# The last block of a two-layer FFN kernel: another order of the last down sums, smaller last stores, and smaller down-weight loads

## The chip, the cores and the metric

The kernel runs on one core of one Trainium2 chip. The metric is the device time of one execution in microseconds; where a kernel was timed several times, the median of its runs.

A core has five engines with queues of their own: TensorE (PE in the profile; its weight loads are listed as PEld), VectorE (DVE), ScalarE (ACT), GpSimd (POOL) and SyncE (SP). Transfers are issued here from the queues of SP, ACT and POOL and are moved by 16 DMA engines.

## The reference, cut to what matters

Two layers, each a residual around a feed-forward network whose input is first transformed per batch. All the change touches is the last product of the second layer and the final sum:

```python
def _L1_ffn_ref(x, ln_w, gate_w, up_w, down_w):
    var = jnp.mean(jnp.square(x), axis=-1, keepdims=True)
    nx = x * jax.lax.rsqrt(var + RMS_EPS) * ln_w
    g = jnp.einsum('bsh,ih->bsi', nx, gate_w)
    u = jnp.einsum('bsh,ih->bsi', nx, up_w)
    return jnp.einsum('bsi,hi->bsh', jax.nn.silu(g) * u, down_w)
x = x + _L0_ffn_ref(_L0_cond_ref(x, ...), ...)
x = x + _L1_ffn_ref(_L1_cond_ref(x, L1_cond_weight, itok_B_3_7), L1_ffn_ln_w, ...)
return x
```

x has 8 batches of 128 tokens with 512 features, 1024 tokens in all; the inner width of the second layer is 1792. The first layer's weights are 4-bit numbers with scales, the second layer's are float32.

## The kernel before, in words

**Layout.** Everything is held transposed: features on the 128 partitions, the 1024 tokens along the free dimension, in two halves tb = 0 and 1 of 512 (TB). The residual and result `xT` has four chunks m of 128 features (KC = 4); the inner width of the second layer is 14 chunks j of 128.

**Products in three sums.** A float32 product is made from reduced-precision (fp32r) parts. Weight and activation are each split into H (high), L (low, scaled) and D (a difference of the two). A bank of PSUM first gets all products of parts 0 and 1 (the H and L sums), is multiplied by a constant in place (`rescale`, lines 174 to 181, which picks ACT or DVE by a planner's account of their load), and then gets the products of part 2 (D) on top. `done` (L1138, on DVE) adds the bank, times a constant, to `xT`.

**Blocks.** The second layer's inner chunks are worked in four blocks, `BLOCKS1` = (0, 4), (4, 8), (8, 11), (11, 14). In each, gate and up (L1056) are made for its chunks j, with the splitting of later weights put between by the planner, then `down(j0, j1)` (matmuls L1121) adds the block's part to all four output chunks. In the middle of a block, `load_down` issues the loads of its down weights on SP (L1103), in pairs of chunks of 512 KB and a single one where the number is odd; `prepare_down` queues their splitting: ACT reads the raw weights (L940, L943), DVE makes the other parts (L949, L952). Loads of gate and up weights (`load_wgu`, L932) go through the same SP queue.

**The order of the work.** The instructions of PE, DVE and ACT run in the order in which the program writes them; each waits by semaphores for what it reads. Transfers from SP and ACT take one of eight completion counters in turn; a transfer that takes a counter again first waits for the one that had it before. At the program's end SP checks the counters one after another, in a fixed order.

**The last block.** With chunks 11 to 13, each sum of H and L over one tb is 2 x 3 = 6 matmuls, each D sum 3. The order of the 72 matmuls is: H and L of output chunks 0, 1, 2 (36 in all, rescaled as they end); D of chunks 0 and 1 (`added`, 6 each), each followed by `done` over 1024 columns and two stores of 512 columns (L1142; tb 0 from ACT's queue, tb 1 from SP's); H and L of chunk 3, tb 0 then tb 1, each with its rescale; D of chunk 2 with `done` and two stores; D of chunk 3 for tb 0, `done`, store; the same for tb 1. The core of it (L1147 and after):

```python
m = KC - 1
banks[m, 1] = pair("down")[:, 1]
for tb in tbs:
    passes(m, (tb,), every, (0, 1))
    rescale(banks[m, tb], HLSCALE)
added(m - 1)
for tb in tbs:
    store(m - 1, tb)
for tb in tbs:
    passes(m, (tb,), every, (2,))
    done(m, xT[:, m, tb * TB : (tb + 1) * TB], banks[m, tb])
    store(m, tb)
```

After the last instruction every engine takes a branch (L1228) over a second version of the network, which inputs of this kind do not need, to the program's end (L1371), where SP checks the counters and the engines meet.

Of the kernel before, what the change touches and what calls it, by code (L numbers as in the profile page):

```python
# [13 lines left out]
F32 = mybir.dt.float32  # L14
# [5 lines left out]
AF = mybir.ActivationFunctionType  # L20
ALU = mybir.AluOpType

P = 128
B, T, D = 8, 128, 512
NT = B * T
TB = 512
# [36 lines left out]
HLSCALE = -(1.0 + EPS) / EPS  # L63
# [32 lines left out]
def network_in(ctx, tc, a, out, by_groups, flag, again):  # L96
    nc = tc.nc
# [4 lines left out]
    def pair(name):  # L102
        return psum.tile([P, 2, 512], F32, tag="ps", name=name)
# [9 lines left out]
    xT = const.tile([P, KC, NT], F32, name="xT")  # L113
# [19 lines left out]
    def charge(engine, us):  # L133
        load[engine] = max(load[engine], clock[0] + AFTER) + us

    def took(engine, n):

        return 0.1 + n / 1000 if engine == "act" else 0.15 + n / 950
# [29 lines left out]
    def spent(n):  # L168

        base = clock[0]  # L170
        clock[0] += 0.2326 * n
        pump(base, clock[0] + OVER)

    def rescale(ps, by):
        n = ps.free_size()
        engine = min(load, key=lambda e: max(load[e], clock[0] + AFTER) + took(e, n))
        charge(engine, took(engine, n))
        if engine == "act":
            nc.scalar.activation(ps, ps, AF.Copy, scale=by)  # L179
        else:  # L180
            nc.vector.tensor_scalar(ps, ps, by, None, ALU.mult)
# [39 lines left out]
    for b in range(B):  # L221
        (nc.scalar, nc.sync)[b % 2].dma_start(
            out=xb[:, b].rearrange("p c t -> p (c t)"), in_=a["xb"][b]
# [7 lines left out]
    at = np.cumsum((0,) + SMALLS)  # L231
# [221 lines left out]
    def by_groups_of_scales():  # L453
# [243 lines left out]
        with tc.manual_schedule(engines={EngineType.PE, EngineType.DVE, EngineType.Activation}):  # L697
# [64 lines left out]
            pools["w1"] = w1_stack.enter_context(tc.tile_pool(name="w1", bufs=1, side="right"))  # L762
            hp = h_stack.enter_context(tc.tile_pool(name="h0", bufs=1, side="right"))
            load_down(*BLOCKS0[0])
            for pair0 in PAIRS0[2:4]:
                load_qw(*pair0)
# [17 lines left out]
            gate_up_pair(2, 3)  # L784
            flush("d0")
            load_down(*BLOCKS0[1])
            dequantise(PAIRS0[3])
            queue_down(*BLOCKS0[1], "d4", at=clock[0] + 6.0)
            down(*BLOCKS0[0])
            ready(PAIRS0[2])  # L790
            load_qw(*PAIRS0[4])
            gate_up_pair(4, 5)
            ready(PAIRS0[3])
            load_qw(*PAIRS0[5])
            flush("d4")
            load_down(*BLOCKS0[2])
            dequantise(PAIRS0[4], (8, 10))
            gate_up_pair(6, 7)
            dequantise(PAIRS0[5], (10, 11))
            queue_down(*BLOCKS0[2], "d8")  # L800
            queue("dve", "indices", 1.7, indices)
            down(*BLOCKS0[1])
            flush("indices")
            first_w1()
# [291 lines left out]
            queue_split(f"h{j}", h, h3[j])  # L1096

    def load_down(j0, j1):
        raws = {}
        for k0 in range(j0, j1, 2):  # L1100
            k1 = min(k0 + 2, j1)
            raws[k0, k1] = fd.tile([P, 2, D], F32, tag="wd", bufs=2, name="wd1")[:, : k1 - k0]
            nc.sync.dma_start(out=raws[k0, k1], in_=a["wd1"][:, k0:k1, :])  # L1103
        return raws

    def prepare_down(raws):
# [6 lines left out]
    def down(j0, j1):  # L1113

        sums = [pair("down") for _ in range(KC)]
        banks = {(m, tb): sums[m][:, tb] for m in range(KC) for tb in range(NTB)}
        last = j1 == NJ1

        def one(m, tb, j, which):
            for i in which:  # L1120
                nc.tensor.matmul(  # L1121
                    banks[m, tb],
                    lhsT=d3[j][i][:, m * P : (m + 1) * P],
                    rhs=h3[j][i][:, tb],
                    start=(i == 0 and j == j0),
                    stop=(j == j1 - 1 and i != 0),
                    skip_group_check=(i == 2),
                )
            spent(len(which))

        def passes(m, tbs, js, which):
            for tb in tbs:
                for j in js:
                    one(m, tb, j, which)

        def done(m, x, ps):
            charge("dve", took("dve", ps.free_size()))
            nc.vector.scalar_tensor_tensor(x, ps, -EPS, x, ALU.mult, ALU.add)  # L1138

        def store(m, tb):  # L1140
            cols = slice(tb * TB, (tb + 1) * TB)
            (nc.scalar, nc.sync)[tb].dma_start(out=out[m * P : (m + 1) * P, cols], in_=xT[:, m, cols])  # L1142

        tbs, every = range(NTB), range(j0, j1)

        def first(m):
            passes(m, tbs, range(j0, j1 - 1), (0, 1))  # L1147

        def ended(m):

            passes(m, tbs, range(j1 - 1, j1), (0, 1))
            rescale(sums[m], HLSCALE)

        def added(m):
            passes(m, tbs, every, (2,))
            done(m, xT[:, m, :].rearrange("p (b t) -> p b t", b=NTB), sums[m])

        if last:


            for fn in (first, ended):
                for m in range(KC - 1):
                    fn(m)
            for m in range(KC - 2):
                added(m)
# [3 lines that stand above are left out]
            banks[m, 1] = pair("down")[:, 1]  # L1169
            for tb in tbs:  # L1170
                passes(m, (tb,), every, (0, 1))
                rescale(banks[m, tb], HLSCALE)
            added(m - 1)
            for tb in tbs:
                store(m - 1, tb)
            for tb in tbs:
                passes(m, (tb,), every, (2,))
                done(m, xT[:, m, tb * TB : (tb + 1) * TB], banks[m, tb])
                store(m, tb)
            return  # L1180
        for fn in (first, ended, added):
            for m in range(KC):
                fn(m)

    with tc.manual_schedule(engines={EngineType.PE, EngineType.DVE, EngineType.Activation}):
        for j0, j1 in BLOCKS1:
            for j in range(j0, j1):
# [6 lines left out]
                if j == 0:  # L1194
# [5 lines left out]
                    fd = ctx.enter_context(tc.tile_pool(name="fd", bufs=1, side="left"))  # L1200
# [12 lines left out]
            if j1 == NJ1 and by_groups:  # L1213

                again.append(nc.values_load(flag[:1, :], min_val=0, max_val=1))
                tc.mark_branch_hint_location("again", hint=again[0], engines=FETCHED)
            down(j0, j1)


# [156 lines left out]
```

## Time and profile before

| what | value |
|---|---|
| median of 3 runs | 436.3 us (435.57 to 436.6) |
| the profiled execution's own time | 436.83 us |
| its span, from first to last instruction | 434.9 us |
| mean granted TensorE clock | 0.996 |
| PE busy | 424.8 us (98%), 1855 matmuls |
| DVE busy | 302.4 us (70%) |
| ACT busy | 232.0 us (53%) |
| down matmuls of layer 2 (L1121) | 336, 76.8 us, 389 ns each |
| transfers | 33.07 MB, 76 GB/s over the span |
| out stores (L1142) | 8 of 256 KB; 2.5 / 3.4 / 4.0 us to landing (least, median, most) |
| wd loads (L1103) | 6 of 512 KB (3.7 us to landing), 2 of 256 KB (2.6 us) |

The page belongs to one execution; its engines' rows give busy time, its chain the work that ended last, followed back from the end. A matmul lasts 389 ns but they overlap, so busy PE is not the same as PE at its peak. Times with a decimal point and no other mark are microseconds from the start of the span.

### The profile page before, as it was taken

The page shows a single profiled execution, that of the slowest core. Times are in us where ns is not written, and L with a number is a line of the kernel's source. Part 1 is how long each engine was busy: PE and PEld are TensorE (multiplying, and loading weights), DVE is VectorE, ACT ScalarE, POOL GpSimd, SP SyncE. Part 2 cuts the span into 40 slices and gives each one's busy share as a digit, 9 for nine tenths or more (in the row PEclk, how much of TensorE's full clock was granted, in tenths as well). Part 3 has the DMA queues.
Part 4 walks back from the last instruction along what each step waited for, and adds up shares of the span by engine and source line. Part 5 has one row for each costly group of instructions (what it writes and reads, how often), then busy time and mean ns, then how long its engine had stood idle before and what let it go on. Part 6 is the DMA issues. An engine that isn't in the chain of part 4 may idle for free.

```text
span 434.9 us, 4847 instructions
## 1 busy us (share of the span) xinstructions
PE 424.8 (98%) x1855; PEld 334.5 (77%) x1855; DVE 302.4 (70%) x432; ACT 232.0 (53%) x269; POOL 9.0 (2%) x20
## 2 busy tenths in 40 slices
PE   8999999999999999999999999999999999999992
PEld 8875778888888764447888888888888888888882
DVE  3998979998998769768179634679334676725552
ACT  5923899678877765347478132484132471425420
POOL 1000000000002001100000000000000000000000
PEclk9999999999999999999999999999999999999998
DMA  8931301010001505842114101132001110000013
GB/s 290 344 150 49 98 0 50 18 37 2 0 2 48 242 6 204 301 167 83 64 50 145 48 2 48 50 97 72 2 0 48 50 48 26 0 0 2 2 53 146
DMA packets 12094, 33.07 MB, mean 76 GB/s; under 512 B 1568, under 2 KB 4256, under 8 KB 11040
## 3 DMA queue, kind: packets, MB, share of 16 engines
q1 hardware_dynamic: 9760, 22.21, 15.3%
q0 software_dynamic: 1152, 8.39, 5.1%
q10 hardware_dynamic: 1152, 2.10, 1.3%
q8 instruction: 16, 0.26, 0.2%
q14 instruction: 14, 0.11, 0.1%
HBM read 30.59 MB, written 2.10 MB: 75 GB/s over the span
## 4 chain that ended last, share of the span: by engine, by line
PE 91%; DVE 4%; DMA 2%; ACT 1%; issue 0%; SPq 0%; ACTq 0%; DVEq 0%
PE gate L1056 18%; PE up L1056 18%; PE down L1121 17%; PE gate L539 9%; PE down L587 8%; PE up L539 8%; PE base L390 5%; PE adapt L999 5%; PE base L416 2%; DMA xb<-in_xb 2%; PE experts L293 1%; DVE xT L599 1%; PE nxT L1019 1%; ACT sl L555 1%; DVE h L558 1%; DVE w L952 1%
## 5 line engine op out<-in xcount | busy, mean ns | idle before, releaser
L1056 PE MATMUL gate<-a,w 128*128 128x512 f32 x336 | 81.8, 390 | 0.0
L1056 PE MATMUL up<-a,w 128*128 128x512 f32 x336 | 81.4, 389 | 0.0
L1121 PE MATMUL down<-h,d 128*128 128x512 f32 x336 | 76.8, 389 | 0.0
L1056 PEld LDWEIGHTS up<-a,w 128*128 128x128 f32 x336 | 63.1, 188 | 13.2
L1121 PEld LDWEIGHTS down<-h,d 128*128 128x128 f32 x336 | 63.1, 188 | 13.1
L1056 PEld LDWEIGHTS gate<-a,w 128*128 128x128 f32 x336 | 62.7, 188 | 13.5 <-ACT gate L179 0.6
L1073 DVE SCALAR_TENSOR_TENSOR h<-up,sl 128x1024 f32<-128x1024 f32 (+1 forms) x16 | 17.5, 1092 | 51.0 <-PE up L1056 44.6
L539 PE MATMUL gate<-a,dq 128*128 128x512 f32 (+1 forms) x176 | 47.7, 393 | 0.1
L539 PE MATMUL up<-a,dq 128*128 128x512 f32 (+1 forms) x176 | 47.4, 391 | 0.0
L587 PE MATMUL down<-h,wd 128*128 128x512 f32 (+1 forms) x176 | 42.3, 393 | 0.6 <-DVE h L193 0.4
L587 PEld LDWEIGHTS down<-h,wd 128*128 128x128 f32 (+1 forms) x176 | 32.5, 188 | 9.5 <-DVE h L193 0.9
L539 PEld LDWEIGHTS gate<-a,dq 128*128 128x128 f32 (+1 forms) x176 | 32.4, 185 | 8.4 <-ACT sl L555 0.6
L539 PEld LDWEIGHTS up<-a,dq 128*128 128x128 f32 (+1 forms) x176 | 32.4, 185 | 7.9 <-DVE a L671 0.3
L203 ACT ACTIVATE h<-h 128x1024 fp32r<-128x1024 f32 (+1 forms) x25 | 26.4, 1054 | 15.9 <-DVE h L1073 15.5
L1070 ACT ACTIVATE sl<-gate 128x1024 f32<-128x1024 f32 (+1 forms) x16 | 14.7, 919 | 35.8 <-PE gate L1056 35.8
L193 DVE TENSOR_TENSOR h<-h,h 128x1024 fp32r<-128x1024 f32 (+1 forms) x25 | 30.5, 1218 | 3.4 <-ACT h L203 3.4
L179 ACT ACTIVATE gate<-gate,ratio 128x1024 f32<-128x1024 f32 (+1 forms) x24 | 26.1, 1086 | 10.6 <-PE gate L539 10.6
L179 ACT ACTIVATE gate<-gate 128x1024 f32<-128x1024 f32 (+1 forms) x15 | 13.8, 923 | 30.8 <-PE gate L1056 30.8
L999 PE MATMUL adapt<-w,xT 128*128 128x512 f32 x64 | 28.9, 597 | 0.0
L179 ACT ACTIVATE down<-down 128x1024 f32<-128x1024 f32 (+1 forms) x10 | 9.2, 923 | 35.8 <-PE down L1121 35.8
L179 ACT ACTIVATE up<-up,ratio 128x1024 f32<-128x1024 f32 (+1 forms) x23 | 25.0, 1085 | 4.9 <-PE up L539 4.9
L1138 DVE SCALAR_TENSOR_TENSOR xT<-down,xT 128x1024 f32<-128x1024 f32 (+1 forms) x17 | 19.6, 1161 | 9.3 <-PE down L1121 9.1
(137 smaller groups left out, 482.6 us busy)
## 6 DMA issues: line engine op xcount, KB each, us to landing
wgu<-in_wgu SPq DMA_DIRECT2D x14, 512.0 KB, 3.3
wd<-in_wd SPq DMA_DIRECT2D x6, 512.0 KB, 3.7
qw<-in_qw_gu SPq DMA_DIRECT2D x5, 512.0 KB, 4.2
xT<-in_xT SPq DMA_DIRECT2D x2, 1024.0 KB, 11.6
xb<-in_xb ACTq DMA_DIRECT2D x4, 256.0 KB, 5.6
xb<-in_xb SPq DMA_DIRECT2D x4, 256.0 KB, 6.1
wT<-in_WT SPq DMA_DIRECT2D x4, 256.0 KB, 5.9
qwd<-in_qw_d SPq DMA_DIRECT2D x2, 512.0 KB, 8.2
```

Of the source, the lines that this page charges most:

```text
L179: nc.scalar.activation(ps, ps, AF.Copy, scale=by)
L193: nc.vector.tensor_tensor(lo, x, hi.bitcast(F32), ALU.subtract)
L203: nc.scalar.activation(hi, x, AF.Copy, scale=HSCALE)
L390: nc.tensor.matmul(base[m], lhsT=wT3[i][:, m, c * P : (c + 1) * P], rhs=x_parts(tb)[i][:, c, :], start=(i == 0 and c == 0), stop=(i == 1 a ...
L539: nc.tensor.matmul(ps, lhsT=dqs[j][:, c, half, :], rhs=a3[i][:, c, tb * TB : (tb + 1) * TB], start=(c == 0 and i == 0), stop=(i == 1), ski ...
L587: nc.tensor.matmul(ps[:, tb], lhsT=wds[k][:n, m * P : (m + 1) * P], rhs=h2[k][i][:, tb], start=(first and i == 0), stop=(i == 1), skip_gro ...
L999: nc.tensor.matmul(ps, lhsT=xT[:, c, b * T : (b + 1) * T], rhs=wt[:, c * D : (c + 1) * D], start=(c == 0), stop=(c == KC - 1),)
L1056: nc.tensor.matmul(ps, lhsT=w3[j][i][:, c, half * P : (half + 1) * P], rhs=a3[i][:, c, tb * TB : (tb + 1) * TB], start=(i == 2 and c == 0) ...
L1070: nc.scalar.activation(sl, ps, AF.Silu, scale=1.0 + EPS)
L1073: nc.vector.scalar_tensor_tensor(h, ps, 1.0 + EPS, sl, ALU.mult, ALU.mult)
L1121: nc.tensor.matmul(banks[m, tb], lhsT=d3[j][i][:, m * P : (m + 1) * P], rhs=h3[j][i][:, tb], start=(i == 0 and j == j0), stop=(j == j1 - 1 ...
L1138: nc.vector.scalar_tensor_tensor(x, ps, -EPS, x, ALU.mult, ALU.add)
```

## The change

Three edits, all in the second layer's `down`:

1. In the last block the D sum of output chunk 2 (with its `done` over 1024 columns) moves up, between the H and L sums of chunk 3 for tb 0 and those for tb 1. Its stores are issued after both. The two scalings of chunk 3 are written for ACT and no longer chosen by the planner.
2. The last output chunk is finished and stored in four pieces of 256 columns instead of two of 512. The queues of the stores are exchanged: tb 0 goes from SP, tb 1 from ACT.
3. The down weights of all blocks but the first are loaded one chunk (256 KB) at a time instead of in pairs; the tiles, and the instructions that read them, stay in pairs.

```diff
     def load_down(j0, j1):
         raws = {}
+        n = 2 if j0 == 0 else 1
         for k0 in range(j0, j1, 2):
             k1 = min(k0 + 2, j1)
-            raws[k0, k1] = fd.tile([P, 2, D], F32, tag="wd", bufs=2, name="wd1")[:, : k1 - k0]
-            nc.sync.dma_start(out=raws[k0, k1], in_=a["wd1"][:, k0:k1, :])
+            raw = raws[k0, k1] = fd.tile([P, 2, D], F32, tag="wd", bufs=2, name="wd1")[:, : k1 - k0]
+            for k in range(k0, k1, n):
+                nc.sync.dma_start(out=raw[:, k - k0 : k - k0 + n], in_=a["wd1"][:, k : k + n, :])
         return raws
...
-        def store(m, tb):
-            cols = slice(tb * TB, (tb + 1) * TB)
-            (nc.scalar, nc.sync)[tb].dma_start(out=out[m * P : (m + 1) * P, cols], in_=xT[:, m, cols])
+        def store(m, i, n=TB):
+            cols = slice(i * n, (i + 1) * n)
+            engine = (nc.sync, nc.scalar)[i * n // TB]
+            engine.dma_start(out=out[m * P : (m + 1) * P, cols], in_=xT[:, m, cols])
...
             banks[m, 1] = pair("down")[:, 1]
             for tb in tbs:
                 passes(m, (tb,), every, (0, 1))
-                rescale(banks[m, tb], HLSCALE)
-            added(m - 1)
-            for tb in tbs:
-                store(m - 1, tb)
+                nc.scalar.activation(banks[m, tb], banks[m, tb], AF.Copy, scale=HLSCALE)
+                if tb == 0:
+                    added(m - 1)
+            for t in tbs:
+                store(m - 1, t)
+            n = TB // 2
             for tb in tbs:
                 passes(m, (tb,), every, (2,))
-                done(m, xT[:, m, tb * TB : (tb + 1) * TB], banks[m, tb])
-                store(m, tb)
+                for i in range(TB // n):
+                    at = tb * TB + i * n
+                    done(m, xT[:, m, at : at + n], banks[m, tb][:, i * n : (i + 1) * n])
+                    store(m, at // n, n)
             return
```

## The prediction

> **What bounds the kernel now.** I read the busy slices of the page first, then the chain that ended last, then the last 15 us in small windows, then the single transfers and sequencer records behind the last vector operation.
>
> ```profile
> PE   8999999999999999999999999999999999999992
> PEclk9999999999999999999999999999999999999998
> DMA  8931301010001505842114101132001110000013
> ```
>
> ```profile
> 428.30:431.00 2.70, 0.00 (x0) 0.00 (x0) 0.00 (x0) 0.00 (x0) 0.00 (x0) 1.00 0.93 338
> 431.00:434.90 3.90, 0.00 (x0) 0.00 (x0) 0.00 (x0) 0.00 (x0) 0.00 (x0) 0.58 0.03 12
> ```
>
> By the page's 40 slices TensorE is full at a full clock until the last slice. The two rows of the windows table (length; busy time of PE, PEld, DVE, ACT, POOL; clock; DMA share; GB/s) show the rest: from 428.3 no engine computes, for 2.7 us the transfers run at 338 GB/s, and then 3.9 us pass with almost nothing moving. So the main part is worth nothing here unless it breaks, and the tail is 6.65 us long (428.3 to the span's end, 434.95).
>
> ```profile
> 410.81 14.97 PE down L1121 x66
> 425.78 0.03 issue
> 425.81 0.02 DVEq L1138
> 425.83 0.04 issue
> 425.87 1.39 DVE xT L1138 x2
> 427.26 0.35 issue
> 427.61 0.68 DVE xT L1138
> ```
>
> In the chain (start, length, what), 66 of the last 72 matmuls run without a gap, and then DVE ends it: the last six matmuls (to 427.12) hide behind DVE's 128x1024 addition of the third chunk. The last addition ends at 428.29.
>
> ```profile
> L1142 SPq DMA_DIRECT2D out<-xT x4: 332/335/348, 421.7 to 428.3; - x4
> L1142 ACTq DMA_DIRECT2D out<-xT x4: 338/369/382, 421.7 to 427.7; - x4
> DMA to landing us min/median/max: 2.5/3.4/4.0
> ...
> L1228 SPq EVENT_SEMAPHORE  x8: 17/17/17, 431.4 to 432.8; - x8
> L1228 ACTq COMPARE_BRANCH  x1: 68/68/68, 428.1 to 428.1; - x1
> L1228 DVEq EVENT_SEMAPHORE  x1: 21/21/21, 430.8 to 430.8; - x1
> L1228 ACTq EVENT_SEMAPHORE  x1: 17/17/17, 431.5 to 431.5; - x1
> ```
>
> Eight stores of 256 KB. Four are issued between 427.13 and 428.32: 1 MB is pending at once, and the DMA engines are saturated to 430.75, with two of the 16 late. The last store, issued at 428.32, lands at 432.29, the 4.0 of the row. SP's eight checks (431.4 to 432.8) are of the eight counters that the transfers take in turn: it waits for the second of them at 432.31, walks through the other six until 432.77, then through its other checks, and the span ends 2.66 us after the landing. Beside this, each engine leaves by a branch: ACT's is at 428.10 and its next instruction comes only at 431.55, 3.45 us later (DVE: 427.18 to 430.78, 3.60).
>
> **Part by part.** Times are on the trace's clock. Matmuls here start every 0.227 us; the third chunk's six D matmuls become numbers 55 to 60 of the 72 instead of 61 to 66.
>
> *Third chunk earlier.* Its last matmul ends at 424.41 instead of 425.77 (6 x 0.227 = 1.36). DVE has been idle since 422.95, starts the addition 0.1 later, ends at 425.73 instead of 427.10. Its two stores are no longer pending together with the last chunk's: SP issues at 425.76; ACT's sits behind ACT's second scaling and issues by 426.4 (bounds 425.86 and 426.4; it matters little). At the traced rate 512 KB take 1.4 us, from about 426.6 to 428.0.
>
> *A wait added.* Before, nine matmuls (2.04 us) lay between the end of tb1's H and L sums and its D; now three do. ACT starts scaling 0.04 us after the last H/L matmul, as at 424.44: 425.80, and takes 0.58, to 426.38. The weight load of tb1's first D waits for it, and its matmul follows 0.22 us after the load starts: 426.65 instead of 426.29. TensorE waits 0.37 us (bounds: 0.1 if the load were ahead, 0.5 with a slow semaphore) and ends at 427.50. Behind it are only tb1's three matmuls, DVE's two pieces, two stores.
>
> *Four additions for two.* 1024 columns take 1.225 us and 512 take 0.68, so 256 take about 0.41; starts are 1.14 and 0.60 apart, so pieces of 256 start 0.34 apart. Tb0: 426.55 and 426.89, to 427.30. Tb1: 427.57 and 427.91, to 428.32. Before: 428.29. The wait eats what the shorter DVE queue had gained: computing ends even, by 0.03.
>
> *Stores.* SP takes tb0's pieces (427.0, 427.33, both over before the next). ACT takes tb1's two: at its 0.37 per issue, 428.01 and 428.43, the second held 0.05 by the first and by a check of a counter, done at 428.80; its branch comes at 428.83. Before: SP at 428.32, ACT's branch 428.10. One issue more than before on each queue, so the last is issued 0.11 later. From issue to first packet was 0.82 (421.69 to 422.50): 429.25. A packet of 1,024 bytes takes 0.046 in this trace's records against 0.084 for 2,048; eight an engine are 0.37: 429.62. From last packet to landing 0.45: 430.07. The late engines carried 8 KB instruction fetches of 0.31 to 0.41 us each, and were 0.3 to 1.1 late; I keep 0.3 to 0.8: 430.4 to 430.9, where it was 432.29.
>
> Here a rule speaks against cutting. The trace has the 0.046 above. The Trainium skill, "DMA: Bandwidth & Descriptors", section Bandwidth, measured on loads of another issue path, advises transfers of 1 MiB or more[...]: 0.95 us for 64 KB, 6.15 for 1 MB. Between them 128 KB would be 1.30 (an estimate from that page). Two in a row from 428.83 would end at 431.4, land at 431.9, and the sum would be about -0.9 instead of the -1.3 below. I take the trace's, since its packets of exactly this size were timed here.
>
> *Single chunks of the down weights.* Blocks 2, 3 and 4 issue 4, 3, 3 loads instead of 2, 2, 2: four issues of 0.33 us more on SP, four more landings. Their cover: the loads at 233.78, 242.0, 288.2, 296.4, 353.5 and 361.1 are first read by ACT at 283.1, 289.4, 348.4, 350.4, 397.3 and 399.4, 36 us or more later, and the gate/up loads behind them in SP's queue (234.9, 289.3) are read at 273.9 and 322.1. Cost nothing; without that cover 0.33 us per issue. But the eight DMA counters go round in turn. Four transfers more shift the ten stores so that the last takes the eighth counter of SP's walk, not the second. The six checks behind it (432.31 to 432.75, 0.45 us) are then done while the last store is under way.
>
> *The way out.* By the landing: 430.4 to 430.9 plus 2.66 - 0.45 = 2.2 gives 432.6 to 433.1. By SP: its branch at 427.7, at most 2.68 us (428.70 to 431.38) until its checks, eight of them 0.6, then 2.15: 433.1. By ACT: 428.83 + 3.45 = 432.28; SP checks ACT's counter 1.39 us before the end (433.56 against 434.95): 433.7. DVE: about 427.7 + 3.6, checked 1.54 before the end, 432.9. ACT's exit is the longest. Its 3.45 is bounded above by DVE's 3.60; TensorE's branch was answered in at most 2.09, and then SP's 433.1 decides. I take 3.45, the row of the same engine.
>
> Sum: 433.7 against 434.95 is -1.25. The profiled execution took 436.83 (1.9 around its span) and would take 435.6; it lies 0.5 above the median 436.3 of the three runs, which becomes 435.0.
>
> **The rivals.**
>
> *The store's own latency binds (same).* For it: the best landing of 256 KB, on an idle queue, was still 2.5 us, and the two instruction fetches could hit the same late engine again. Against it: half the bytes and nothing queued. If the last store takes 3.5 us as the median does, it lands at 431.95, and with 2.2 the end is 434.15: -0.8; with a late engine on top, -0.3. The same follows if the counters do not turn as I count them. About 435.8.
>
> *ACT is late at tb1's scaling (slower).* That scaling had 1.3 us to spare and has none now; whatever holds ACT there goes whole into TensorE, DVE, the last store and ACT's own exit. Its place is between 425.8 and 426.4, its price a break in ACT's instruction supply like the 3.45 at the branch: +3.45 - 1.25 = +2.2, 438.5. It decides from a hold of 1.3 us; by 0.2% from 2.1. Against it: in the trace of before ACT follows its last matmul by 0.04 us there, and a store issue of 0.37, as held the first scaling until 423.40, is too short.
>
> *The split loads do harm (slower by little).* A gate/up load late behind them would open TensorE; the least slack behind a split load is over 30 us, so I give it little.
>
> *The change's sums do not come earlier.* If the D of the third chunk waited for its own scaling nothing would move; that scaling ended at 420.07, 2.8 us before.
>
> **How the numbers follow.** What a measurement of this kernel can tell from no change is about 0.2%, 0.87 us. Main case: 0.73, 435.0, itself 433.9 (landing path, counter gain, quick exit) to 435.4. Latency case: 0.14, 435.4 to 436.8. ACT late: 0.09, split loads 0.04. From the main case 0.72 and from the second 0.04 are faster by over 0.2%; the rest of the second is same; the last two are slower. The range 433.9 to 436.7 takes in the first two and leaves the slow ones out.
>
> **What would show it.** In the profile of after: the third chunk's addition at about 424.5; a gap of about 0.37 us in TensorE before the last three matmuls, with ACT's scaling as releaser; four additions of about 0.41, the last ending near 428.3; out stores of 128 KB with a shortest landing near 2 us; no stretch over 2 us at 338 GB/s after computing ended; ACT's first instruction after its branch near 432.3 and SP's last counter check at the landing. Wrong if the last landing is after 431.5, if TensorE waits much longer than 0.5 us, or if any gap opens before 410.

## The result, and the profile after

The changed kernel took 434.84 us (median of 8 runs, 434.57 to 436.36) against 436.54 us for the kernel before (8 runs): a ratio of 0.9966, 95% interval [0.9954, 0.9977], which is 1.5 us less, between 1.0 and 2.0. The forecast was 435.0. Its profiled execution took 434.81 us with a span of 433.0 us.

The part of the program ahead of the last block has the same matmuls in all kernels here, and in each of the profiled executions the last 799 of them take 181.11 us. Yet the first down matmul of the last block starts anywhere from 409.6 to 411.7 us. So this scatter arises earlier, before the first of the split down loads, and the time goes with it: the execution that starts the block at 409.63 lies 1.3 us under its kernel's median, the one that starts it at 411.74 lies 1.8 us over. Everything below is therefore counted from that matmul ("block time"): 410.64 in the profile of before, 410.44 in that of after. By block time the end moved from 24.31 to 22.58 us: -1.73.

A store leaves sixteen completion updates in the record. They are read here as one from each of the 16 DMA engines; the store has landed with the last of them. An engine is called late when its update comes well after most others, and an issue held when it takes longer than the usual 0.33 to 0.41 us.

The chain of the changed kernel, from its end (start, length, what):

```profile
410.60 16.61 PE down L1125 x72
427.21 0.02 issue
427.24 0.10 DVE xT L1142
427.34 0.24 issue
427.58 0.41 DVE xT L1142
```

All 72 matmuls are now in the chain, and DVE follows the last one at once. In the 16.61 us TensorE waits once, which the group of ACT's scalings shows under those who waited for it; the second view has the last nine matmuls (least/median/most in ns):

```profile
L1178 ACT ACTIVATE down<-down x2: 582/582/582, 423.2 to 425.6; 128x512 f32<-128x512 f32 x2
...
  PEld down L1125: 0.4, 1
```

```profile
L1125 PE MATMUL down<-h,d x9: 388/389/499, 424.7 to 426.8; 128*128 128x512 f32 x9
```

The 0.4 is the idle time of the weight loads. The matmul that waited starts 0.381 us after the one before it instead of 0.227 and lasts 0.499 instead of 0.389, and the next one starts 0.337 after it. So the last matmul starts at block time 16.36 instead of 16.09, and 0.27 us are lost. Computing ends at block time 17.55 instead of 17.65.

The stretches after it (length; PE, PEld, DVE, ACT, POOL; clock, DMA share, GB/s), the same as shown of before:

```profile
428.30:431.00 2.70, 0.00 (x0) 0.00 (x0) 0.00 (x0) 0.00 (x0) 0.00 (x0) 0.73 0.46 143
431.00:434.90 3.90, 0.00 (x0) 0.00 (x0) 0.00 (x0) 0.00 (x0) 0.00 (x0) 0.50 0.01 4
```

The pile is gone: 143 GB/s where there were 338. But the transfers are not over early; they trickle. The issues and the branches (least/median/most in ns; PEld's branch is TensorE's):

```profile
L1148 SPq DMA_DIRECT2D out<-xT x5: 332/338/411, 421.5 to 427.2; - x5
L1148 ACTq DMA_DIRECT2D out<-xT x5: 339/371/1322, 421.5 to 428.1; - x5
DMA to landing us min/median/max: 2.3/2.8/3.6
...
L1239 SPq EVENT_SEMAPHORE  x8: 17/17/17, 428.1 to 431.2; - x8
L1239 PEldq COMPARE_BRANCH  x1: 412/412/412, 426.2 to 426.2; - x1
L1239 SPq COMPARE_BRANCH  x1: 45/45/45, 427.6 to 427.6; - x1
L1239 ACTq COMPARE_BRANCH  x1: 68/68/68, 429.5 to 429.5; - x1
L1239 ACTq EVENT_SEMAPHORE  x1: 17/17/17, 432.1 to 432.1; - x1
```

And TensorE's branch in before, for the later argument:

```profile
L1228 PEldq COMPARE_BRANCH  x1: 412/412/412, 425.1 to 425.1; - x1
```

ACT's last issue took 1.32 us. SP's eight counter checks now end with the last landing (431.21 and 431.23). The last landing is at block time 20.77 instead of 21.65 (-0.88), and from it to the end it takes 1.81 us instead of 2.66 (-0.85). So half of the gain is an earlier landing and half a shorter closing.

| kernel | computing ends | last landing | end | landing to end | ratio to before |
|---|---|---|---|---|---|
| before | 17.65 | 21.65 | 24.31 | 2.66 | 1 |
| changed | 17.55 | 20.77 | 22.58 | 1.81 | 0.9966 [0.9954, 0.9977] |
| order only | 17.48 | 20.95 | 23.61 | 2.66 | 0.9971 [0.9961, 0.9981] |
| pieces only | 17.78 | 21.76 | 24.18 | 2.42 | 0.9998 [0.9990, 1.0006] |
| single chunks only | 17.65 | 21.59 | 23.43 | 1.84 | 0.9980 [0.9973, 0.9988] |
| changed, weights in pairs | 17.55 | 20.75 | 23.17 | 2.42 | 0.9976 [0.9968, 0.9985] |
| before, eight SP loads more | 17.65 | 21.60 | 23.74 | 2.14 | 0.9983 [0.9976, 0.9990] |
| changed, no second network | 17.55 | 19.62 | 20.52 | 0.90 | 0.9900 [0.9885, 0.9914] |
| changed, pieces in turn | 17.55 | 20.78 | 22.49 | 1.71 | 0.9966 [0.9953, 0.9979] |
| changed, two pieces | 17.49 | 20.68 | 22.52 | 1.84 | 0.9966 [0.9951, 0.9981] |
| halves | 17.27 | 20.66 | 22.40 | 1.74 | 0.9953 [0.9939, 0.9966] |
| halves, pieces in turn | 17.27 | 20.72 | 22.42 | 1.70 | 0.9946 [0.9930, 0.9962] |
| halves, two pieces | 17.21 | 20.50 | 22.34 | 1.84 | 0.9949 [0.9932, 0.9965] |

Block times in us, from one profiled execution each; the ratios are from the timed runs.

### The profile page after: what moved, and what is told of

It reads as the page before. It is cut to its first block, busy times and chain, and to the rows that moved or that the text cites. A ratio compares the mean times of both kernels' runs of the same rounds, so it can differ in the third digit from the quotient of the medians.

```text
span 433.0 us, 4865 instructions
## 1 busy us (share of the span) xinstructions
PE 425.2 (98%) x1855; PEld 335.0 (77%) x1855; DVE 302.6 (70%) x434; ACT 232.1 (54%) x269; POOL 9.0 (2%) x20
## 4 chain that ended last, share of the span: by engine, by line
PE 94%; DVE 3%; ACT 1%; issue 0%; ACTq 0%
PE gate L1056 18%; PE down L1125 18%; PE up L1056 18%; PE gate L539 9%; PE down L587 8%; PE up L539 8%; PE base L390 5%; PE adapt L999 5%; PE experts L293 2%; PE base L416 2%; DVE xT L599 1%; PE idle L246 1%; PE nxT L1019 1%; ACT sl L555 1%; DVE h L558 1%; DVE w L952 1%
## 5 line engine op out<-in xcount | busy, mean ns | idle before, releaser
L1056 PEld LDWEIGHTS gate<-a,w 128*128 128x128 f32 x336 | 62.7, 188 | 13.5 <-ACT gate L179 0.6
L181 DVE TENSOR_SCALAR down<-down 128x1024 f32<-128x1024 f32 x7 | 8.6, 1232 | 23.8 <-PE down L1125 23.8
```

The costliest lines, as they stand in the source:

```text
L1056: nc.tensor.matmul(ps, lhsT=w3[j][i][:, c, half * P : (half + 1) * P], rhs=a3[i][:, c, tb * TB : (tb + 1) * TB], start=(i == 2 and c == 0) ...
```

## The experiments

**One part at a time: the order.**

```diff
                 passes(m, (tb,), every, (0, 1))
-                rescale(banks[m, tb], HLSCALE)
-            added(m - 1)
+                nc.scalar.activation(banks[m, tb], banks[m, tb], AF.Copy, scale=HLSCALE)
+                if tb == 0:
+                    added(m - 1)
```

> Only the order: the D sum of the third chunk between the last chunk's H and L sums, scalings on ACT; two stores of 256 KB for the last chunk from the old queues, down weights in pairs. Theory (the stores piled up, the order separates them): about 435.2 us, -1.3 from before; the third chunk's addition near 424.3, the last store issued near 428.0 and landing at 430.4 to 430.9 instead of 432.29; TensorE waits about 0.15 us. Rival (the size of the last store decides): at most -0.5 us, last landing after 431.5.

Measured 435.35 us, -1.3 (between 0.8 and 1.7). Its profiled execution took 436.65 us, over a microsecond above its median (its block started at 411.26), but by block time landing moved by -0.70, 0.17 of it because the last store is issued earlier, and the closing not at all. The tail of this one execution thus shows only about half of the timed gain; what the rest is, the scatter ahead of the block or more, is open. TensorE loses 0.27 as in the changed kernel, not 0.15, and the last issue at 17.51 is near where it should be (428.0 less 410.64 is 17.4). The landing is not: 430.4 to 430.9 would be 19.8 to 20.3, and it is 20.95, which on the clock of before is 431.6 and on the rival's side of 431.5. Thirteen of the last store's sixteen engines have landed by 19.51, where in before they had by 20.53; three are 1.1 to 1.4 us later. So the pile cost about 0.85 us beside the earlier issue, and late engines take a part of it back.

**The pieces.**

```diff
-                done(m, xT[:, m, tb * TB : (tb + 1) * TB], banks[m, tb])
-                store(m, tb)
+                for i in range(TB // n):
+                    at = tb * TB + i * n
+                    done(m, xT[:, m, at : at + n], banks[m, tb][:, i * n : (i + 1) * n])
+                    store(m, at // n, n)
```

> Only the four pieces of the last chunk (tb 0 from SP, tb 1 from ACT), in the old order of the sums, weights in pairs. Theory of the pile: the third chunk's 512 KB is still issued at 427.1 and pending with the last chunk's, DMA saturated to 430.7, last landing 431.5 or later, time within 0.4 us of before. Rival (the size decides): -0.8 us or more, last landing before 431.

Nothing in sum, as the theory of the pile has it: 0.9998, last landing at 21.76. Two parts of it cancel: computing ends 0.13 later, and the end comes 2.42 after the landing instead of 2.66, since two stores more leave four counter checks behind it instead of six. The counter-test is further down: the changed kernel with two pieces is as fast as with four.

**The single chunks of the down weights.**

```diff
+            n = 2 if j0 == 0 else 1
+            for k in range(k0, k1, n):
+                nc.sync.dma_start(out=raw[:, k - k0 : k - k0 + n], in_=a["wd1"][:, k : k + n, :])
```

> Only the down weights of blocks 2 to 4 in single chunks. Theory (the counters turn): landing of the last store as before, near 432.3, but on the sixth of SP's eight checks, so two checks of about 0.075 us behind it instead of six: -0.3 us, about 436.2. Rival (the loads themselves matter): the start of the last block moves from 410.6 by more than 0.3 us, or nothing changes at the end.

The landing stayed (21.59), but the gain is 0.87 us, between 0.5 and 1.2: more than the counters' 0.3. SP's closing at the program's end shows the rest, first of before, then of this kernel:

```profile
L1371 SPq EVENT_SEMAPHORE  x14: 17/28/28, 432.8 to 434.9; - x14
L1371 SPq DRAIN  x3: 7/7/116, 434.0 to 434.4; - x3
```

```profile
L1373 SPq EVENT_SEMAPHORE  x14: 17/28/28, 431.6 to 433.1; - x14
L1373 SPq DRAIN  x3: 7/7/13, 432.3 to 432.6; - x3
```

From the first of these checks to the first drain it is 1.1 us in before and 0.7 here, with twelve checks in both. In the records of before SP stands still for 0.37 us between its last check (433.56, done 433.58) and the drain (433.96), and the drain takes 0.12 instead of 0.01. In this kernel there is no such pause. My reading was that four more SP transfers had moved the place where SP's next block of code is fetched: before and the other kernels with pairs up to here have an 8 KB instruction fetch 13.5 us into the last block, and this kernel and the changed one have a fetch about 47 us ahead of the block instead (362.4 and 363.1). The records do not tell which engine fetches, and in before no fetch lies in the pause.

> The changed kernel with the down weights in pairs again. Theory (counters): the last store takes the fourth of SP's eight checks, four checks behind it, +0.3 us on the landing side, of which up to 0.1 is hidden because ACT's way out ended together with SP's checks: 0.2 us over the changed kernel, about -1.3 from before. Rival (ACT's way out alone sets the end): no difference from the changed kernel.

435.51 us and an end at 23.17: 0.59 by block time over the changed kernel instead of 0.2. The four checks are there (the last landing is seen at 20.77, the eighth counter at 21.05), and so is the pause, of 0.37 us again, now three checks further forward: 1.17 us from the eighth counter to the check of ACT's counter, where it is 0.75 in the changed kernel.

**Only the place in SP's instructions.** To part the two effects, the kernel before with eight SP loads more, a full turn of the counters:

```diff
-        nc.sync.dma_start(out=wgus[j], in_=a["wgu1"][j])
+        n = KC if j < NJ1 - 8 else KC // 2
+        for c in range(0, KC, n):
+            nc.sync.dma_start(out=wgus[j][:, c : c + n], in_=a["wgu1"][j][:, c : c + n])
```

> The kernel before, with the gate and up weights of the last eight chunks loaded in two halves each: eight SP transfers more, so the eight counters stand as in the kernel before and six checks lie behind the last landing, but SP's later instructions lie eight places further on. Theory (half of what single chunks gave is SP's code being fetched earlier): SP goes on within about 0.5 us of its branch instead of 2.7, the pause of 0.4 us in SP's closing is gone, the end comes 2.2 to 2.3 us after the last landing instead of 2.66, about -0.4 us. Rival (only the counters matter): 2.66 us and the time of before.

The pause is gone, and so is the fetch at 13.5; one lies 76.5 us ahead of the block instead. The end comes 2.14 us after the landing, with six checks still between: 0.9983. So of the closing's 0.82 that single chunks save (2.66 to 1.84), about 0.5 comes from the place of SP's later instructions and 0.3 from the counters, four checks of 0.075. That the place works through SP's code fetches fits the fetches' times, but is argued and not shown. That SP would go on within 0.5 us of its branch could not be seen: its first counter belongs here to a store that lands at 20.84, and it goes on at 20.86.

**The late engines and the held issue.** First the last pieces from the two queues in turn:

```diff
-            engine = (nc.sync, nc.scalar)[i * n // TB]
+            engine = (nc.scalar, nc.sync)[i % 2]
```

> The changed kernel with the last chunk's pieces from ACT, SP, ACT, SP in turn. Theory (the last issue of 1.32 us was held by two pieces back to back on one queue): every issue takes about 0.34 to 0.41 us, the last at about 17.6 us after the block's start, last landing at about 20.3 instead of 20.8; ACT's branch 1.5 us earlier; -0.4 us from the changed kernel. Rival (late DMA engines hold any issue then): the last issue, now SP's, takes 0.7 to 1.3 us, landing as in the changed kernel.

Neither fits whole. All issues are short, as the theory has it, and the last starts at 17.58:

```profile
L1148 SPq DMA_DIRECT2D out<-xT x5: 332/333/348, 420.7 to 427.2; - x5
L1148 ACTq DMA_DIRECT2D out<-xT x5: 338/346/382, 420.7 to 426.9; - x5
DMA to landing us min/median/max: 2.4/2.8/3.5
```

Yet the last landing is at 20.78 as in the changed kernel: thirteen engines have landed by 19.44, three at 20.4 to 20.8. By these two executions the held issue cost nothing, and the late engines set the landing; the timed ratio is the same too (0.9966). Then the same changed kernel without the second version of the network and the branch over it:

```diff
-                again.append(nc.values_load(flag[:1, :], min_val=0, max_val=1))
-                tc.mark_branch_hint_location("again", hint=again[0], engines=FETCHED)
...
-    with tc.If(again[0] > 0, preferred_fallthrough_block=True, label="again", name="again"):
-        network(tc, a, out, False)
```

> The changed kernel without the second version of the network and the branch over it (it leaves out only the code for other inputs). Theory (instruction fetches at the branch make some DMA engines late and set the engines' ways out): no fetches of 8 or 16 KB between the last stores, no landing over 0.4 us behind the others of its store, last landing at 19.8 to 20.2 us after the block's start instead of 20.8, end 0.7 to 1.2 us earlier than in the changed kernel. Rival (the engines are late of themselves): the same late landings, and less than 0.3 us.

```profile
L1148 SPq DMA_DIRECT2D out<-xT x5: 332/343/413, 422.8 to 428.5; - x5
L1148 ACTq DMA_DIRECT2D out<-xT x5: 338/377/413, 422.8 to 429.4; - x5
DMA to landing us min/median/max: 1.9/2.5/3.5
```

The order of work is that of the changed kernel, and the issue that took 1.32 us takes 0.41. The sixteen engines of each of the last four stores land within 0.22 us of each other, the last at 19.62, a little earlier than expected. The DMA queues of the end (packets, MB, share): first the two instruction queues of the changed kernel, then all that this one has:

```profile
q14 instruction: 5, 0.04, 1.7%
q8 instruction: 1, 0.02, 0.7%
```

```profile
q10 hardware_dynamic: 470, 0.57, 24.2%
q1 hardware_dynamic: 435, 0.53, 22.2%
```

Here no instruction fetch is among the last stores; in the changed kernel there are one of 16 KB (block time 17.59) and three of 8 KB (18.34, 18.42, 19.96). So the lateness of the engines, and the hold, go with the branch and its fetches, which this edit takes out together.

The stores of the first two output chunks part them, with no branch near. In five kernels an 8 KB fetch runs at block time 13.5 (before, order only, pieces only, changed with weights in pairs, and this one), in eight it does not. ACT's second store, issued at 12.34 in all, lands at 15.8 in the five, its last engine 0.62 to 0.67 us behind the fifteenth; in the eight it lands at 15.1, no engine over 0.03 behind. So a single fetch goes with a late engine.

The end came 2.06 us earlier, not 0.7 to 1.2, because the engines' ways out and the first eight checks of SP are gone with the branch: 0.90 us from landing to end. The timed runs, 0.9900 against 0.9966, give 2.9 us; the rest does not lie in the last block.

**Better covers.** The third chunk's D sum cut by tb, so that six matmuls lie over ACT's second scaling:

```diff
-                if tb == 0:
-                    added(m - 1)
+                passes(m - 1, (tb,), every, (2,))
+                done(m - 1, xT[:, m - 1, tb * TB : (tb + 1) * TB], banks[m - 1, tb])
```

> The changed kernel with the third chunk's D sum cut by tb: three D matmuls and an addition of 512 columns after each tb's H and L sums of the last chunk. Six matmuls then lie over ACT's second scaling: theory: no gap in TensorE's last block (0.227 between starts), computing ends 0.15 us earlier; TensorE's branch and its 16 KB instruction fetch come earlier by about 0.7 us or more and meet fewer of the last stores. -0.2 to -0.5 us from the changed kernel. Rival: the third chunk's second store goes out 0.7 us later and takes the gain back; same as the changed kernel.

The gap is gone (0.227 throughout), computing ends 0.28 earlier, TensorE's branch 0.68 earlier. The end is only 0.18 earlier: the 16 KB fetch, at 16.25, now falls among the pieces of tb 0, three issues are held (1.24, 0.96, 0.62 us), and the landing is at 20.66.

With two pieces instead of four (`n = TB`), without and with the halves, and with halves and pieces in turn:

> The changed kernel with the last chunk in two stores of 256 KB (SP, ACT). Theory (late DMA engines, not the size of the last store, set the last landing): landing as in the run of the order alone, about 20.9 us after the block's start against 20.8, and two counter checks behind it (0.15): 0.2 us over the changed kernel. Rival (the four pieces carry part of the gain): landing at 21.3 or later, 0.5 us or more over the changed kernel.

> Both variants together: the third chunk's D sum cut by tb, and the last pieces from ACT, SP, ACT, SP. Theory (late engines set the landing): all issues under 0.45 us, thirteen of the last store's sixteen engines landed by 19.3 us after the block's start, the last at 20.3 to 20.7, time within 0.3 us of the variant with halves alone. Rival (the held issues of that variant cost its gain): 0.4 us or more below it, last landing before 20.2.

> The variant with halves, and the last chunk in two stores of 256 KB. Theory (late engines): last landing 20.5 to 20.9 us after the block's start, two checks behind it, within 0.3 us of the changed kernel. Rival (fewer, larger stores meet the instruction fetches better): 0.3 us or more below the changed kernel, last landing before 20.3.

Two pieces are as fast as four: 0.9966 both, landing 20.68, and no issue over 0.38 us. With halves and pieces in turn, issues were held again, against the expectation (1.28, 0.92, 0.65), and no engine of the last store has landed by 19.3; the landing is at 20.72:

```profile
L1148 SPq DMA_DIRECT2D out<-xT x5: 332/348/1282, 421.9 to 428.9; - x5
L1148 ACTq DMA_DIRECT2D out<-xT x5: 338/372/921, 421.9 to 427.8; - x5
```

With halves and two pieces the landing, 20.50, is as expected. Of the kernels that keep the branch, the three with halves have the lowest medians, 434.35 to 434.58, ratios 0.9946 to 0.9953; their intervals overlap that of the changed kernel, so they beat the kernel before, and the changed one perhaps. Between them the runs do not choose.

## Why the prediction was right, and where its steps were off

The direction and the size held (435.0 against 434.84), by the mechanism named first: the third chunk's stores no longer pend together with the last chunk's. The order alone shows it, and the single chunks turned the counters as counted: the last landing is on SP's last check. But several terms were off and partly cancelled, so that the number came so close is in part luck.

- *Third chunk earlier.* Right: the addition comes at 13.87 by block time, 1.36 us earlier. Only the rate is misread: 512 KB at the 338 GB/s shown take 1.55 us, not 1.4. Nothing in the sum rests on it.
- *The wait added.* Forecast 0.37 us, measured 0.27. ACT's scaling ends where forecast (block time 15.74). The working let the first matmul start 0.22 after its weight load, as in a stream. After the wait the records have both start together (426.234 and 426.236), but this matmul is 0.11 longer and the next one comes as much later, so only half of the 0.22 is saved.
- *Stores.* Forecast: last landing at 430.4 to 430.9, by block time 19.8 to 20.3. Measured 20.77. The path without fetches was nearly right: 430.07 is 19.43, and without the branch 19.62 was measured. The term for late engines, 0.3 to 0.8, was too small: in the third of the four pieces, whose issue was not held, three engines are 1.2 to 1.4 behind the other thirteen. The sign named for it, a store of 128 KB that lands near 2 us after its issue, came only without the branch (1.9); here the shortest is 3.1. The term was read from before, where a 16 KB fetch (block time 15.57) fell into the pause between two bursts of stores. I take this fetch for TensorE's, since it follows TensorE's branch by 1.1 to 2.1 us in all kernels that have one. The branch in turn follows ACT's last scaling by 0.05 to 0.06 us. (TensorE's sequencer branches before its last matmuls have run: in before they end at 16.48.) The scaling now ends 1.36 later, so the branch moves from 14.44 to 15.79 and the fetch among the last stores (17.59). What a moved engine triggers elsewhere was not followed.
- *Four additions for two, pieces.* Forecast as even for computing, measured 0.10 earlier. The small size was given 0.3 us of packets; the runs give it nothing that can be told.
- *Single chunks.* The loads cost nothing, as forecast: the 799 matmuls ahead of the block take the same time. Their gain was put at 0.45, and then hidden behind ACT's way out. It is 0.85 of closing in the changed kernel: 0.45 of checks and about 0.5 from the place of SP's later instructions, less 0.10 that SP waits for ACT. Most of the 0.5 was in the trace of before, as SP's pause between its last check and its drain, but was carried along in "1.39 before the end" as if it were fixed.
- *The way out.* ACT's was named as the last one, and is, by 0.1 us: SP's check of ACT's counter waits until 432.10. ACT's first instruction after its branch came where forecast, at block time 21.61 against 21.64, but by luck: the branch is 0.85 later (19.04 against 18.19, the held issue), and the answer takes 2.57 instead of 3.45. From SP's check of ACT's counter, once it is through, to the end is 0.92 instead of 1.39. This is what makes the end 1.73 earlier and not 1.25.

Of the rivals, the store's own latency did not bind: the last store went from issue to landing in 3.1 us, and 1.9 was possible without fetches. ACT was not late at tb1's scaling (it follows TensorE by 0.04), and the split loads moved nothing ahead of the last block. The batching rule of the Trainium skill ("DMA: Bandwidth & Descriptors", section Bandwidth), weighed in the prediction, would have had the last two pieces take 2.6 us (the estimate of 1.30 from that page, twice); here four pieces and two are equally fast, and without fetches the last two pieces landed 0.46 us apart, the last 1.9 us after its issue.

Open: why an issue is held by 0.6 to 1.3 us in some kernels and not in others. Without the fetches at the branch it is not. With them it is in all kernels with four pieces but one (pieces in turn, without halves), and in none with two. Which engines are late could not be seen, since the records name a packet's queue and not its engine; so that the late ones are those that carried a fetch, as the prediction has it, is not shown.

## What to carry to other kernels

When the last compute ends well before the span does, read the end by itself: which transfers pend together, in which order their completions are checked, and which instruction fetches fall among them. Separating the stores in time was worth more than cutting them smaller. And a change that adds or drops a few transfers anywhere moves the turn of the completion counters and the place of an engine's later instructions, so a difference of half a microsecond need not come from what was edited.

## What was not expected of the hardware

- Instruction fetches run beside the stores on the DMA engines. The 16 KB packet took 0.93 us in the trace of before, the 8 KB ones in its last block 0.31 to 0.44. With them some engines of the last stores landed up to 1.6 us behind the others; without them none landed over 0.22 after the first. The Trainium skill, "Runtime: NRT & Kernel Launch", section Instruction fetch mechanics, says that a taken branch to code that is not at hand stalls the engine for the fetch; in these traces ACT took 2.6 to 3.6 us from its branch to its next instruction.
- The issue of a store, 0.33 to 0.41 us, can take 1.3 us beside such fetches.
- Eight more transfers in a full turn of the counters, the last of them 91 us ahead of the end, made the kernel before 0.7 us faster (0.4 to 1.0): SP's pause of 0.37 us near the end was gone, and a fetch had moved out of the last block.
